# A decoder layer on one core: the order of the first loads, the place of attention's constants, and when the clearing of slots begins

## The chip, the cores and the metric

The kernel runs on one NeuronCore of a Trainium2 chip. A core has five engines with a queue each: PE (TensorE, matmuls; the load of its weights is shown as PEld), DVE (VectorE), ACT (ScalarE), POOL (GpSimd) and SP (SyncE, which here only hands out transfers). Sixteen DMA engines move the data. The metric is the time of one execution on the device in microseconds, lower is better. The span is the time from the first to the last instruction of the profiled execution.

## The reference

Input x has 8 sequences of 512 tokens with 512 numbers each, all in float32; a context of the same shape and a mask come with it. Three sublayers follow each other, and after each its output is added to its input and normalised without parameters:

```
x = norm(x + ssm(x))         # state space layer
x = norm(x + xattn(x, ctx))  # cross-attention, 16 heads of 32
x = norm(x + moe(x))         # 32 experts, 4 per token, plus a shared MLP
```

The state space layer is what matters for the beginning. It normalises x with ln_w and ln_b, multiplies by in_proj_w (512 x 2048) into a main half and a gate z, convolves each of the 1024 channels over four tokens (conv_w, conv_b) and applies SiLU. x_proj_w makes of that a step size dt and the vectors B and C of 16 states. Then, for each channel and state, `h = exp(A dt) h + dt B x`, with `A = -exp(A_log)`, runs over all tokens of the sequence, and `y = sum(h C) + D x` is gated with SiLU(z), multiplied by out_proj_w and by res_scale, and added to x.

Cross-attention projects with Wq, Wk, Wv, Wo and the biases bq, bk, bv, bo; masked positions get a score of -1e8. The experts each take at most 640 tokens (CAP): a token's rows go into slots, and rows beyond are dropped.

## The kernel before

The program has three parts after one another: `layers` (state space layer, attention and gate), `experts`, and `finish` (the last norm).

`layers` works in 16 chunks of T = 256 tokens, two for each sequence (`chunks`). Within a chunk there are 32 steps (`steps`, counted by k): four pairs of channel blocks q, four groups of states g, two blocks. A step makes decays on ACT (`decays`, L438), multiplies on DVE with a broadcast of B (`scan`, L450), scans on DVE (L454), multiplies with a broadcast of C (`collect`, L471) and sums over states on PE (L475). The broadcasts are the tiles `bc`, which SP fetches from a small scratch in DRAM (`bcast`, L379). Into these steps the code weaves other work by their number k: the output of the chunk before (`back`), the gate's projection (`gate_x`), the next chunk's input (`load_x` at k = 5, `norm_x` at 9, `flip_x`, `convolve`, `x_proj`), and a list `side` of attention's work for the sequence before, popped by weights.

Before the first chunk's steps there is a front with nothing to weave it into: load x, normalise it (`norm_x`), transpose (`flip_x`), four times project and convolve (`convolve`, with the matmuls in `project`, L303, the copy in L323 and the taps in L329 and L337), SiLU, the projection to dt, B and C (`x_proj`, L360, spilled to DRAM by L368), the preparation of dt (`prepare`), its spreading to both halves of the partitions (L419), the broadcasts, and the first decays.

The weights of the projections come in pieces of 512 KB through three buffers (`wm`, from the generator `pieces`). Its first `next` asks for two pieces and gives the first; every later one asks for one more and gives the one asked for before. In `before` the generator starts in the first `project`.

Constants are loaded by `const` (L128), one transfer on SP's queue each, and A_log by 16 small transfers (L149). `aneg` is made of it on ACT and DVE (L153, L154). Attention's constants follow: bq is scaled (L166), qa, ka and va get rows of ones and zeros (L206 to L213), the mask becomes a fill (L217 to L221), and bv goes through Wo into bo: a copy of bv's columns (L974), eight matmul instructions in the profile (L975), a sum (L978). `clear` (L235 to L240) writes one expert's 640 slots from a tile `zero` with one transfer of 1362.5 KB; it is called 32 times, at every odd k of the first two chunks (L1091). All transfers named here are on SP's queue.

The code's order is not the order on the engines. When the program is built, a planner runs it against assumed costs: each engine takes, whenever it is idle, the ready instruction that stands first in the program. An instruction is ready when its inputs are there and its buffer is free. The order that results is fixed for the chip, where each engine then keeps to it and waits where an input is late. `keep_in_program_order` holds the SiLUs and their table loads in the order written.

Of the kernel before, what the change touches and what calls it, by code (L numbers as in the profile page):

```python
# [1 line left out]

# [14 lines left out]
P = 128  # L17
# [9 lines left out]
T = 256  # L27
# [54 lines left out]
def layers(ctx, tc, a, x1d, filld, based, xbuf):  # L82
# [48 lines left out]
    def rows(w):  # L131
        return w.rearrange("(c p) f -> p c f", p=P)

    lnw = const("lnw", [P, DC], a["ln_w"])
    lnb = const("lnb", [P, DC], a["ln_b"])
    cw = const("cw", [P, CC, 4], rows(a["conv_w"]))
# [8 lines left out]
    for r in range(2):  # L145
        for j in range(2):
            for g in range(NST // NG):
# [17 lines left out]
    bq = const("bq", [P, DC], a["bq"])  # L165
    nc.vector.tensor_scalar(bq, bq, HD**-0.5, None, ALU.mult)  # L166
    bk = const("bk", [P, DC], a["bk"])
    bv = const("bv", [P, DC], a["bv"].rearrange("(c p) -> p c", p=P))
    bo = const("bo", [P, D], a["bo"].partition_broadcast(P))
    wg = const("wg", [P, DC, E], rows(a["wg"]))  # L170


    ones = cp.tile([P, P], F32, name="l_ones")
# [38 lines left out]
    va = cp.tile([P, SC, NH // 2, 3 * HD], F32, name="l_va")  # L212
    nc.gpsimd.memset(va[:, :, :, HD : 2 * HD], 1.0)  # L213


    mu8 = p3.tile([P, D], F32, tag="row", name="mu8").bitcast(U8)[0:B, 0:S]
    nc.sync.dma_start(mu8, a["mask"])  # L217
    fl = p3.tile([P, D], F32, tag="row", name="fl")
    nc.vector.tensor_copy(fl[0:B, :], mu8)
    nc.vector.tensor_scalar(fl[0:B, :], fl[0:B, :], -1.0, 1e8, ALU.add, ALU.mult)  # L220
    nc.sync.dma_start(filld, fl[0:B, :])  # L221

    def big(tag, name):
        return p1.tile([P, SC * (ROW if tag == "s1" else D)], F32, tag=tag, name=name)

# [14 lines left out]
        )  # L240

    def pieces():


        w_in, w_out = rows(a["in_proj_w"]), rows(a["out_proj_w"])
        xs = [w_in[:, :, 2 * q * P : 2 * (q + 1) * P] for q in range(CC // 2)]
        zs = [w_in[:, :, DI + 2 * q * P : DI + 2 * (q + 1) * P] for q in range(CC // 2)]
        outs = [w_out[:, 2 * q : 2 * q + 2, :] for q in range(CC // 2)]  # L250
        n = B * (S // T)
        order = list(xs)
        for i in range(n):
            order += (outs if i else []) + zs + (xs if i + 1 < n else [])
        order += outs
        got = None
        for src in order + [None]:
            nxt = None
            if src is not None:
                nxt = p2.tile([P, 4 * 2 * P], F32, tag="wm", name="wm", bufs=3).rearrange(  # L260
                    "p (c f) -> p c f", c=src.shape[1]
                )
                nc.sync.dma_start(nxt, src)
            if got is not None:
                yield got
            got = nxt
# [440 lines left out]
    def units(b):  # L707
# [258 lines left out]
                add(*sends[j])  # L966
        return todo


    load("Wo")  # L970
    rep = p3.tile([P, D], F32, tag="row", name="rep")
    psb = psm.tile([P, D], F32, tag="mm", name="ps_bo")
    for dc in range(DC):
        nc.vector.tensor_copy(rep[:, dc * P : (dc + 1) * P], bv[:, dc : dc + 1].to_broadcast([P, P]))  # L974
        nc.tensor.matmul(  # L975
            psb, rep[:, dc * P : (dc + 1) * P], loaded["Wo"][:, dc, :], start=(dc == 0), stop=(dc == DC - 1)
        )
# [40 lines left out]
    do(prepare, 0, f)  # L1018
    dry()
    bc, n = bcast(f, 0), 0  # L1020
    decays(0, 0, f["ready", 0][0], das[0])
    old, side = None, []

    for i, (b, t) in enumerate(chunks):
        nf = {}
        after = chunks[i + 1] if i + 1 < len(chunks) else None
        if t == 0:
            side, spent = units(b - 1) if b else sources(0), 0.0

            own = [work(k) for k in range(len(steps))] * 2  # L1030
            whole = sum(own) + sum(x[0] for x in side)
        py = None
        for k, (q, g, ci) in enumerate(steps):
            if ci == 0:
                if (q, g) != (CC // 2 - 1, NST // NG - 1):
                    bcn = bcast(f, (g + 1) % (NST // NG))
                else:
                    bcn = bcast(nf, 0) if after else None
            h = carry(t, 2 * q + ci, g)

            if k + 1 < len(steps) or after:
# [24 lines left out]
            if after:  # L1066
                if k == 5:
                    load_x(*after, nf)
                if k == 9:
                    norm_x(nf)  # L1070
                if k == 11:
                    for j in range(DC // 2):
                        do(flip_x, j, nf)
                if k in (12, 15, 18, 21):
                    do(convolve, after[1], (k - 12) // 3, nf, first=(k == 12))
                if k == 23:
                    dry()
                    silu(*nf["xs"].values())
                if k == 24:
                    do(x_proj, nf)  # L1080
            if side and (k >= 3 or t and k == 0):
                at = t * len(steps) + k + 1
                while side and spent + sum(own[:at]) <= whole * at / len(own):
                    w, fn, alone = side.pop(0)
                    spent += w
                    do(fn, first=alone)
            settle()
            collect(2 * q + ci, g, h, bc, py, f)
            if ci == 1:
# [330 lines left out]
```

## Time and profile before

| | |
|---|---|
| median of three runs | 5591.53 us (5585.55 to 5597.78) |
| profiled execution | 5587.21 us, span 5585.2 us |
| granted PE clock | 0.938 of full speed |
| PE busy | 4864.8 us (87% of the span) |
| DVE busy | 4348.3 us (78%) |
| ACT busy | 2589.2 us (46%) |
| moved by DMA | 769.83 MB, 138 GB/s on average |

The profile is one execution. Its slices cut the span into 40 equal stretches of 140 us; a digit is the busy share of an engine in tenths. In a timeline, a line gives start and duration in us, engine, line of the code, operation, what it writes and reads, and how many alike were merged; in brackets stands how long the engine was idle before, and what ended that. For a transfer ("SPq") the duration is that of handing it out on SP, not of the movement. In a view of waits, the numbers are us in total, times, and the longest.

### The profile page before, as it was taken

The numbers are of one execution on the slowest core, as the hardware profiler recorded it, in microseconds if no ns is written. First come the engines' busy times: TensorE is split into PE (matmuls) and PEld (weight loads), VectorE is DVE, ScalarE is ACT, GpSimd is POOL, SyncE is SP. The second block draws the span as 40 slices with busy tenths as digits, with TensorE's granted clock in tenths as the row PEclk, the third lists the DMA queues.
The fourth block names the chain that finished last, engine by engine and source line by source line (L and its number), as shares of the span: only waits on it lengthen the run. The fifth ranks groups of instructions, "written<-read, shape, count | busy, mean of one in ns | idle before, by whom it ended". The sixth has DMA issues, their size and how long they took to land. (4 is left out here: it accounts for less than half of the span.)

```text
span 5585.2 us, 60354 instructions
## 1 busy us (share of the span) xinstructions
PE 4864.8 (87%) x19752; PEld 2711.8 (49%) x19752; DVE 4348.3 (78%) x5738; ACT 2589.2 (46%) x5481; POOL 565.5 (10%) x424
## 2 busy tenths in 40 slices
PE   5667888888988988888888898889899999999994
PEld 3233344334433434443443343333577777777773
DVE  5998999999889999898989999853566565555554
ACT  4554655565566555565555656523222222222223
POOL 0000002001100200200010020010111111111111
PEclk8778999999999999999999999989999999999997
DMA  7787345444634634543463464431445545454444
GB/s 202 214 230 203 106 130 183 123 115 134 187 105 112 199 103 127 180 129 109 128 199 101 116 189 111 113 118 37 140 124 126 125 125 125 119 126 125 123 115 139
DMA packets 560426, 769.83 MB, mean 138 GB/s; under 512 B 135754, under 2 KB 268394, under 8 KB 560112
## 3 DMA queue, kind: packets, MB, share of 16 engines
q1 hardware_dynamic: 522608, 680.70, 41.6%
q0 software_dynamic: 33280, 76.90, 7.3%
q10 hardware_dynamic: 4224, 8.39, 0.4%
q8 instruction: 156, 2.56, 0.2%
q14 instruction: 158, 1.29, 0.1%
HBM read 508.68 MB, written 165.05 MB: 121 GB/s over the span
## 5 line engine op out<-in xcount | busy, mean ns | idle before, releaser
L438 ACT ACTIVATE l_da<-both,l_aneg 128x256 f32<-128x256 f32 x2048 | 889.1, 499 | 816.9 <-DVE h L454 775.4
L454 DVE TENSOR_TENSOR_SCAN h<-l_da,h 128x1028 f32<-128x1028 f32 x512 | 1169.8, 2292 | 51.6 <-ACT h L444 29.6
L475 PE MATMUL py<-h,l_twice 128*64 128x256 f32 x4096 | 625.4, 419 | 210.5 <-DVE h L471 210.3
L450 DVE TENSOR_TENSOR h<-both,bc 128x1024 f32<-128x1024 f32 x512 | 617.8, 1214 | 134.4 <-PE py L475 72.0
L471 DVE TENSOR_TENSOR h<-h,bc 128x1024 f32<-128x1024 f32 x512 | 622.4, 1218 | 8.2 <-DMA bc<-scr 2.1
L475 PEld LDWEIGHTS py<-h,l_twice 128*64 128x64 f32 x4096 | 292.5, 146 | 585.9 <-DVE h L471 251.0
L767 PE MATMUL ps_s<-l_ka,l_qa 64*128 64x512 f32 x1024 | 319.3, 703 | 141.7 <-DVE mx L769 141.3
L1200 PE MATMUL ps_h<-xT,w 128*128 128x320 f32 x1536 | 436.1, 434 | 0.0
L1280 POOL DMA_INDIRECT based<-y,xe x160 | 252.2, 1577 | 1314.3 <-ACT y L1303 573.8
L769 DVE TENSOR_REDUCE mx<-ps_s 128x2 f32<-128x1024 f32 x256 | 310.1, 1214 | 82.7 <-PE ps_s L767 81.8
L1221 DVE TENSOR_TENSOR hT<-ps_h,p 128x320 f32<-128x320 f32 x128 | 62.9, 491 | 374.9 <-PE ps_h L1200 374.7
L1200 PEld LDWEIGHTS ps_h<-xT,w 128*128 128x128 f32 x1536 | 292.5, 191 | 118.4 <-issue 0.8
L793 PE MATMUL ps_t<-l_qa,l_ka 64*128 64x512 f32 x1024 | 298.0, 646 | 15.8 <-ACT eT L797 12.1
L797 ACT ACTIVATE eT<-ps_t 128x1024 f32<-128x1024 f32 x256 | 258.7, 1012 | 109.5 <-PE ps_t L793 109.3
L809 PE MATMUL po<-eT,l_va 128*64 128x512 f32 x1024 | 279.2, 623 | 24.4 <-ACT raw L821 19.6
L1200 PE MATMUL ps_h<-t,s 128*128 128x320 f32 x1024 | 286.1, 432 | 0.0
L642 POOL DMA_INDIRECT xbuf<-x2t,dest x128 | 218.3, 1706 | 651.2 <-DVE dest L636 561.8
L704 PE MATMUL ps_p<-x2T,wa 128*128 128x512 f32 x512 | 245.5, 629 | 12.9 <-DVE hT L884 10.7
L303 PE MATMUL ps_z<-xnT,wm 128*128 128x256 f32 x1024 | 240.9, 388 | 15.4 <-DVE o L513 13.0
L303 PE MATMUL ps_x<-xnT,wm 128*128 128x256 f32 x1024 | 240.8, 389 | 3.2 <-ACT dt L401 1.9
L504 PE MATMUL po<-wm,zs 128*128 128x512 f32 x512 | 233.3, 605 | 3.3 <-DMA wm<-in_out_proj_w 1.8
L1200 PEld LDWEIGHTS ps_h<-t,s 128*128 128x128 f32 x1024 | 194.6, 190 | 81.1
(225 smaller groups left out, 7401.3 us busy)
## 6 DMA issues: line engine op xcount, KB each, us to landing
bc<-scr SPq DMA_DIRECT2D x1024, 128.0 KB
w<-in_w SPq DMA_DIRECT2D x96, 1024.0 KB
wm<-in_in_proj_w SPq DMA_DIRECT2D x128, 512.0 KB
xbuf<-zero SPq DMA_DIRECT2D x32, 1362.5 KB
xe<-xbuf SPq DMA_DIRECT2D x32, 1362.5 KB
both<-dt SPq DMA_DIRECT2D x256, 128.0 KB
both<-dtx SPq DMA_DIRECT2D x256, 128.0 KB
wm<-in_out_proj_w SPq DMA_DIRECT2D x64, 512.0 KB
```

The lines of the kernel that those rows point to most:

```text
L303: nc.tensor.matmul(ps[:, i, :], w[:, dc, i * P : (i + 1) * P], f["xnT"][:, dc, :], start=(dc == 0), stop=(dc == DC - 1),)
L438: nc.scalar.activation(da[:, n, 1:], dt[:, c % 2, j, :], AF.Exp, scale=aneg[:, c, j, g, m : m + 1])
L450: nc.vector.tensor_tensor(steps, dtx[:, c % 2].unsqueeze(2).to_broadcast([P, 2, NG // 2, T]), bc[0], ALU.mult)
L454: nc.vector.tensor_tensor_scan(flat, da.rearrange("p n t -> p (n t)"), flat, 0.0, ALU.mult, ALU.add)
L471: nc.vector.tensor_tensor(steps, steps, bc[1], ALU.mult)
L475: nc.tensor.matmul(py[j * HP : (j + 1) * HP, c % 2, :], twice, h[:, j * 2 + m, 1:], start=False, stop=(s == (NST // NG - 1, NG // 2 - 1, 1)),)
L767: nc.tensor.matmul(ps[:, j, :], qa[r, lt * P : (lt + 1) * P], ka[r, :], start=True, stop=True)
L769: return lambda: nc.vector.tensor_reduce(mx[:, lt, :].unsqueeze(2), ps, AX.X, ALU.max) and None
L793: nc.tensor.matmul(ps[:, j, :], ka[r, kc * P : (kc + 1) * P], qa[r, :], start=True, stop=True)
L797: nc.scalar.activation(eT, ps, AF.Exp)
L809: nc.tensor.matmul(po[j * 2 * HD : (j + 1) * 2 * HD, :], va[:, kc, i, j * HD : (j + 2) * HD], eT[:, j, :], start=(kc == 0), stop=(kc == SC ...
L1200: nc.tensor.matmul(ps, w[:, n, r * P : (r + 1) * P], x[:, n, :], start=not more and n == 0, stop=n == 1, skip_group_check=more,)
```

## The change

Four things move; no instruction's work changes.

1. x of the first chunk is the first transfer, and the generator of weight pieces is started right after it (`begun`), so that two pieces of in_proj_w come second and third. All constants follow, attention's five (bq to wg) directly behind A_log. The first chunk uses the tile loaded so.
2. `aneg` is made after the first broadcast, before the first decays.
3. The scaling of bq, the mask's fill and the product of bv and Wo go into a function `biases`, called in step 2 of the first chunk; Wo is loaded in step 0.
4. The clearings begin when seven steps of the first chunk are over, and are spread evenly over the rest of the first two chunks, up to its end.

```diff
+    def begun(it):
+        first = next(it)
+        return chain([first], it)
+
+    x0 = p1.tile([P, NT_, D], F32, tag="xt", name="xt")
+    nc.sync.dma_start(x0, a["x"][0, 0:T, :].rearrange("(j p) d -> p j d", p=P))
+    piece = begun(pieces())
     lnw = const("lnw", [P, DC], a["ln_w"])
...
-    nc.scalar.activation(aneg, aneg, AF.Exp)
-    nc.vector.tensor_scalar(aneg, aneg, -1.0, None, ALU.mult)
...
     bq = const("bq", [P, DC], a["bq"])
-    nc.vector.tensor_scalar(bq, bq, HD**-0.5, None, ALU.mult)
     bk = const("bk", [P, DC], a["bk"])
...
-    mu8 = p3.tile([P, D], F32, tag="row", name="mu8").bitcast(U8)[0:B, 0:S]
-    nc.sync.dma_start(mu8, a["mask"])
-    fl = p3.tile([P, D], F32, tag="row", name="fl")
-    nc.vector.tensor_copy(fl[0:B, :], mu8)
-    nc.vector.tensor_scalar(fl[0:B, :], fl[0:B, :], -1.0, 1e8, ALU.add, ALU.mult)
-    nc.sync.dma_start(filld, fl[0:B, :])
...
-    piece = pieces()
...
-    load("Wo")
-    rep = p3.tile([P, D], F32, tag="row", name="rep")
-    psb = psm.tile([P, D], F32, tag="mm", name="ps_bo")
-    for dc in range(DC):
-        nc.vector.tensor_copy(rep[:, dc * P : (dc + 1) * P], bv[:, dc : dc + 1].to_broadcast([P, P]))
-        nc.tensor.matmul(
-            psb, rep[:, dc * P : (dc + 1) * P], loaded["Wo"][:, dc, :], start=(dc == 0), stop=(dc == DC - 1)
-        )
-    nc.vector.tensor_tensor(bo, bo, psb, ALU.add)
+    def biases():
+
+        nc.vector.tensor_scalar(bq, bq, HD**-0.5, None, ALU.mult)
...
-    f = {}
-    load_x(0, 0, f)
+    f = {"xt": x0}
     norm_x(f)
...
     bc, n = bcast(f, 0), 0
+    nc.scalar.activation(aneg, aneg, AF.Exp)
+    nc.vector.tensor_scalar(aneg, aneg, -1.0, None, ALU.mult)
     decays(0, 0, f["ready", 0][0], das[0])
-    old, side = None, []
+    old, side, cleared = None, [], 0
...
+            if i == 0 and k == 0:
+                load("Wo")
+            if i == 0 and k == 2:
+                biases()
...
-            if i < 2 and k % 2:
-                clear(i * E // 2 + k // 2)
+            while i < 2 and cleared < E * (i * len(steps) + k - 6) // (2 * len(steps) - 7):
+                clear(cleared)
+                cleared += 1
```

In `biases`, the lines on the mask and on bv follow as they stood before.

More of the change, by code (lines that the diff above doesn't have):

```diff
@@ L1 @@
 from contextlib import ExitStack
+from itertools import chain
 import concourse.bass as bass
@@ L132, in rows, with pieces @@
         return w.rearrange("(c p) f -> p c f", p=P)
+    def pieces():
+        w_in, w_out = rows(a["in_proj_w"]), rows(a["out_proj_w"])
+        xs = [w_in[:, :, 2 * q * P : 2 * (q + 1) * P] for q in range(CC // 2)]
+        zs = [w_in[:, :, DI + 2 * q * P : DI + 2 * (q + 1) * P] for q in range(CC // 2)]
+        outs = [w_out[:, 2 * q : 2 * q + 2, :] for q in range(CC // 2)]
+        n = B * (S // T)
+        order = list(xs)
+        for i in range(n):
+            order += (outs if i else []) + zs + (xs if i + 1 < n else [])
+        order += outs
+        got = None
+        for src in order + [None]:
+            nxt = None
+            if src is not None:
+                nxt = p2.tile([P, 4 * 2 * P], F32, tag="wm", name="wm", bufs=3).rearrange(
+                    "p (c f) -> p c f", c=src.shape[1]
+                )
+                nc.sync.dma_start(nxt, src)
+            if got is not None:
+                yield got
+            got = nxt
+    def begun(it):
[4 more added lines that the diff above has]
+    piece = begun(pieces())
     lnw = const("lnw", [P, DC], a["ln_w"])
@@ L152, in layers @@
                 )
-    nc.scalar.activation(aneg, aneg, AF.Exp)
-    nc.vector.tensor_scalar(aneg, aneg, -1.0, None, ALU.mult)
+    bq = const("bq", [P, DC], a["bq"])
+    bk = const("bk", [P, DC], a["bk"])
+    bv = const("bv", [P, DC], a["bv"].rearrange("(c p) -> p c", p=P))
+    bo = const("bo", [P, D], a["bo"].partition_broadcast(P))
+    wg = const("wg", [P, DC, E], rows(a["wg"]))
     conv_tail = cp.tile([P, CC, 3], F32, name="l_conv_tail")
@@ L163, in layers @@
         nc.gpsimd.memset(da[:, :, 0:1], 0.0)
-    bq = const("bq", [P, DC], a["bq"])
-    nc.vector.tensor_scalar(bq, bq, HD**-0.5, None, ALU.mult)
[L167 to L170, printed above, removed]
     ones = cp.tile([P, P], F32, name="l_ones")
@@ L240, in clear @@
         )
[L244 to L261, printed above, removed]
-                )
[L263 to L266, printed above, removed]
-    piece = pieces()
     def load_x(b, t, f):
@@ L967, in units @@
         return todo
-    load("Wo")
-    rep = p3.tile([P, D], F32, tag="row", name="rep")
-    psb = psm.tile([P, D], F32, tag="mm", name="ps_bo")
-    for dc in range(DC):
-        nc.vector.tensor_copy(rep[:, dc * P : (dc + 1) * P], bv[:, dc : dc + 1].to_broadcast([P, P]))
-        nc.tensor.matmul(
-            psb, rep[:, dc * P : (dc + 1) * P], loaded["Wo"][:, dc, :], start=(dc == 0), stop=(dc == DC - 1)
-        )
-    nc.vector.tensor_tensor(bo, bo, psb, ALU.add)
+    def biases():
+        nc.vector.tensor_scalar(bq, bq, HD**-0.5, None, ALU.mult)
+        mu8 = p3.tile([P, D], F32, tag="row", name="mu8").bitcast(U8)[0:B, 0:S]
+        nc.sync.dma_start(mu8, a["mask"])
+        fl = p3.tile([P, D], F32, tag="row", name="fl")
+        nc.vector.tensor_copy(fl[0:B, :], mu8)
+        nc.vector.tensor_scalar(fl[0:B, :], fl[0:B, :], -1.0, 1e8, ALU.add, ALU.mult)
+        nc.sync.dma_start(filld, fl[0:B, :])
+        rep = p3.tile([P, D], F32, tag="row", name="rep")
+        psb = psm.tile([P, D], F32, tag="mm", name="ps_bo")
+        for dc in range(DC):
+            nc.vector.tensor_copy(rep[:, dc * P : (dc + 1) * P], bv[:, dc : dc + 1].to_broadcast([P, P]))
+            nc.tensor.matmul(
+                psb, rep[:, dc * P : (dc + 1) * P], loaded["Wo"][:, dc, :], start=(dc == 0), stop=(dc == DC - 1)
+            )
+        nc.vector.tensor_tensor(bo, bo, psb, ALU.add)
     chunks = [(b, t) for b in range(B) for t in range(S // T)]
```

## The prediction, made before the changed kernel was run

> **What bounds the kernel now.** I read the cores view first (one core, span 5585.2 us, granted clock 0.938), then the page's slices, then timelines of one engine at a time over the first 480 us, since every edit lies there. The slices (each digit a tenth of busy time in 140 us):
>
> ```profile
> PE   5667888888988988888888898889899999999994
> DVE  5998999999889999898989999853566565555554
> DMA  7787345444634634543463464431445545454444
> ```
>
> Slice 1 of DVE is half empty and the next ones are full. So the start is a front in which everything waits; then DVE carries chunk after chunk until about 3740 us, and PE the experts after that. The DMA share is highest in the first four slices, where the clearings of slots run. The front in SP's timeline (start, duration, line, transfer, count):
>
> ```profile
> 0.81 0.40 SPq L128 DMA_DIRECT2D l_lnw<-in_ln_w  x1
> 5.34 10.91 SPq L149 DMA_DIRECT2D l_aneg<-in_A_log  x16
> 19.01 4.13 SPq L208 DMA_DIRECT2D l_ka<-l_ones  x6
> 24.14 0.42 SPq L526 DMA_DIRECT2D wa<-in_Wo  x1
> 26.14 0.39 SPq L272 DMA_DIRECT2D xt<-in_x  x1
> 26.58 1.85 SPq L263 DMA_DIRECT2D wm<-in_in_proj_w  x3
> 28.52 3.66 SPq L237 DMA_DIRECT2D xbuf<-zero  x2
> ```
>
> SP hands out 0.4 to 0.7 us per transfer, one after another; x is handed out only at 26.14. DVE's and ACT's timelines show who waits for it:
>
> ```profile
> 31.79 1.29 DVE L73 BATCH_NORM_STATS2 st<-xt 128x6 f32<-128x512 f32 x2 [5.49 <-DMA xt<-in_x]
> 41.97 0.59 ACT L323 COPY xp<-ps_x 128x512 f32<-128x512 f32 x1 [2.90 <-PE ps_x L303]
> 50.25 0.59 ACT L323 COPY xp<-ps_x 128x512 f32<-128x512 f32 x1 [2.37 <-DVE xs L337]
> 55.49 0.59 ACT L323 COPY xp<-ps_x 128x512 f32<-128x512 f32 x1 [3.47 <-DVE xs L337]
> 81.87 2.36 DVE L450 TENSOR_TENSOR h<-both,bc 128x1024 f32<-128x1024 f32 x2 [8.16 <-DMA bc<-scr]
> ```
>
> So: x lands at 31.79; the four convolutions follow at 41.97, 46.11, 50.25 and 55.49; the first scan step begins at 81.87. From there DVE hardly stops. The waits view of DVE from 84 to 270 us, whole:
>
> ```profile
> DVE zs L487 <- PE py L475: 2.4, 2, 2.0
> DVE h L454 <- ACT l_da L438: 0.2, 1, 0.2
> ```
>
> From 270 to 460 it waits 15 us, of that 0.8 for a transfer (xt). So the clearings cost DVE nothing, and a start of the first scan that is so much earlier moves all that follows: nothing later is tied to a clock.
>
> **What the Trainium skill says.** "DMA: Bandwidth & Descriptors", the section on the anatomy of one DMA, gives about 2.0 us plus bytes at 436 GB/s, for GpSimd's transfers; 512 KB would take an estimated 3.2 us. This trace: the 256 KB of `based` and Wo's 1 MB behind it, handed out from 23.74, are used at 29.89 (6.15 us for 1.25 MB); x, 512 KB more, at 31.79. That is 1.9 us per 512 KB and 1.4 us besides, 3.3 us for one piece alone; it agrees. The same page, "Issuing engines are not separate DMA queues", says that all share 16 engines and interleave, so a big transfer ahead delays a small one. "PSUM — Partial Sum Buffer", "Engine vs sequencer instructions", says that ScalarE's, VectorE's and GpSimd's queues are strictly first in, first out, and that matmuls keep program order. That decides what a badly placed bias matmul holds up.
>
> **The change part by part.**
>
> *x and two weight pieces first.* x goes out at 0.81 and lands 3.3 us later, at 4.1, 27.7 us earlier. From x to the first convolution's copy are 41.97 − 31.79 = 10.18 us, so 14.3; the second follows 4.14 us later, at 18.4. The constants that norm and convolution need (lnw, lnb, cw, cb) are handed out by about 5 and land in time.
>
> *The third piece.* Only two pieces go first; the third is asked for in the second projection, behind all constants. SP's queue ahead of it: x 0.43 and two pieces 0.62 each (1.67 us), then what ran from 0.81 to 23.19 (the constants, 16 for A_log, attention's five, six rows of ones: 22.38 us), then `based` 0.40. Mask, fill and Wo no longer stand ahead. So it goes out at 0.81 + 1.67 + 22.38 + 0.40 = 25.3. In the waits view of SP over the first 900 us (total, times, longest), issues wait for older transfers:
>
> ```profile
> SPq L379 <- DMA xbuf<-zero: 22.4, 10, 4.1
> ```
>
> If the ninth to eleventh transfers wait likewise for x and the two pieces (landing at 4.1, 6.0 and 7.9), the queue slips by up to 1.85 us; I take half, so 26.2, landing at 29.5. The trace of before can't show this wait; both ends are 28.6 and 30.5. Its 16 matmuls take 3.72: copy at 33.2 instead of 50.25. The fourth piece is right behind. Before, the fourth copy was 5.24 us after the third, 1.1 of it behind the next chunk's statistics; now 4.14 to 5.24. It stands at 37.4 to 38.5 instead of 55.49: **17.0 to 18.1 us earlier, I take 17.5**. Some 10 of the 27.7 us stay behind the constants.
>
> *Wo and the bias product in chunk 0.* SP, PE, DVE and ACT are not in program order here: clearings that belong to step 1 and step 3 of chunk 0 went out at 28.52, before the first projection. A planner fills an idle engine with whatever is ready, first in the program first. So I expect the biases again in the front. DVE pays 0.16 + 0.41 + 0.41 + 0.61 + 0.69 = 2.28 us (L166, L219, L220, L974, L978). Their cover is DVE's idle time in the front, now above all from 18 to 30 us, and then between convolutions. Without cover all 2.28 fall on the full DVE; I take 0.5, as one instruction may get in the way. PE pays 8 matmuls, 5.48 us (L975). The gap between the fourth projection's end (55.45) and the x-projection (59.26) is 3.8 us; they overhang by 1.7, or by one matmul of 0.7 if the x-projection takes precedence. I take 0.5, between nothing (other gaps) and 1.7. What the matmul is queued ahead of is the x-projection, and everything waits for that.
>
> *aneg's exponential and negation* (0.31 + 0.23) move behind the broadcast; A_log lands at about 20, so idle ACT and DVE hide them, 0.54 if not. The memsets of GpSimd start within its first 11 us as before, needed later. Nothing.
>
> *Clearings.* The same 32 transfers of 1362.5 KB, from step 8 of chunk 0 on, in 57 steps instead of 64; the rates go from one in 2.0 steps to one in 1.8. They are first needed by the scatter of sequence 0's tokens, two chunks later. SP's slow hand-outs (3.66 us for two at 28.52) stood in front of pieces that weren't wanted until 41.97. Cover: the broadcasts are there before DVE wants them. Nothing, with a loss possible (fourth rival).
>
> Sum: 17.5 − 0.5 − 0.5 = **16.5 us**. The profiled execution took 5587.2 (its span and 2.0 us): 5570.7. The median of the runs shown is 4.3 us above it, so I forecast 5575.0.
>
> **Rivals.**
> *The whole shift.* The third piece isn't held up (the planner puts it ahead of constants). Then 27.7 − 1.0 = 26.7 us, 5565. Against: before, SP kept to program order in everything that was ready.
> *PE stands behind the bias matmuls.* Wo now follows three pieces of 512 KB: handed out at about 28, behind 1.5 MB from 26.2: 1.4 + 2.5 MB at 1.9 us per 512 KB = 10.9, landing at 37. If the planner puts the bias matmuls ahead of the fourth projection, that waits till 37 and 5.48 more, 42.6 instead of 33.2; its copy comes 8.9 us later than reckoned. If only ahead of the x-projection, 2 us. Gain about 8: 5583. For: PE can't overtake. Against: the planner knows sizes.
> *The new order gives it back.* Every instruction is planned anew. Against: the pairs of chunks repeat, by SP's hand-outs of x1d, within 2 us (467.5, 468.3, 466.7, 467.8, 468.7); for: the first pair takes 477.9. Gain near 0 to 5: 5589.
> *Slower: broadcasts late behind clearings.* In chunk 1 some 18 clearings instead of 16, at a DMA share of already 0.81 (280 to 460 us). SP waited up to 4.1 us for a clearing without DVE noticing; were DVE's lead used up, each such broadcast would cost 4.1 us. From 16.5 / 4.1, four of them, the gain is gone; from seven on it is slower by more than 0.2% (28.7 − 16.5 = 12.2 us). At ten, 5616. Against: in chunks 0 and 1 no step after the first waited for a broadcast.
>
> **How the numbers follow.** Forecast 0.60 (gains of 12 to 21), whole shift 0.10, PE behind the biases 0.14, given back 0.10, slower 0.06. A measurement of this kernel can tell about 0.2%, 11.2 us, from no change. Faster by more: 0.60 + 0.10 = 0.70; within: 0.14 + 0.10 = 0.24; slower: 0.06. The range of 5564 to 5586 takes in the first three cases, 0.84, with their unknown costs (the slip of 1.85, the overhang, the DVE work); the part outside is the last two.
>
> **What would show it.** x's statistics at about 4 us on DVE; the third piece on SP at 25 to 27 and PE's third projection waiting for it; the fourth copy at about 38; the first multiplication of a step at about 65 instead of 81.87; from there DVE without waits for broadcasts, x1d going out some 16 us earlier in every chunk. Wrong if PE waits for Wo ahead of a projection, if the third piece goes out before the constants, if DVE waits for bc among clearings, or if pairs of chunks change their length.

## The result, and the profile after

The changed kernel takes 5574.55 us, the median of 8 runs (5557.79 to 5579.9), beside 5591.13 us (5585.55 to 5597.78) for the kernel before: a ratio of 0.9965 (of the means), 95% interval 0.9956 to 0.9975; the medians lie 16.6 us apart. It is faster by more than the 0.2% that can be told from no change. Run again beside other kernels (the last experiment) it gave 0.9955 (0.9938 to 0.9971). Its profiled execution took 5579.9 us (span 5578.2), the longest of its runs. The forecast was 5575.0 us. The time was met; the way to it was not, as will be seen: the front gave less than the sum said, and, by the profiles, a part that was priced at nothing made up for it.

The page's slices of the changed kernel (columns as before):

```profile
PE   6768889889888988888888898889899999999994
DVE  6988899999889999898989999854565556555554
DMA  6787455445534634543463464431444444454544
```

DVE's first slice rose from 5 to 6. The shape is otherwise the same, so the change has to be read in the timelines. SP's, of the changed kernel (start, duration of the hand-out, line, transfer, count):

```profile
0.81 0.44 SPq L166 DMA_DIRECT2D xt<-in_x  x1
1.31 1.00 SPq L154 DMA_DIRECT2D wm<-in_in_proj_w  x2
...
3.91 1.68 SPq L129 DMA_DIRECT2D l_cb<-in_conv_b  x1
...
6.11 1.31 SPq L129 DMA_DIRECT2D l_w_dt<-in_dt_proj_w  x1
...
8.89 10.91 SPq L183 DMA_DIRECT2D l_aneg<-in_A_log  x16
...
22.56 4.13 SPq L239 DMA_DIRECT2D l_ka<-l_ones  x6
...
27.24 1.58 SPq L154 DMA_DIRECT2D wm<-in_in_proj_w  x3
28.86 0.50 SPq L523 DMA_DIRECT2D wa<-in_Wo  x1
...
38.04 0.46 SPq L260 DMA_DIRECT2D xbuf<-zero  x1
```

x goes first, and the third piece of weights (first of the three at 27.24) stands behind every constant. SP was held up on the way there: two constants took 1.68 and 1.31 us to hand out instead of 0.58 each, while x and the pieces were still moving. Wo was pulled into the front. So was a clearing, at 38.04: the seven steps in the code did not keep four of the 32 clearings out of the time ahead of the first step. DVE's and ACT's timelines:

```profile
4.76 1.29 DVE L74 BATCH_NORM_STATS2 st<-xt 128x6 f32<-128x512 f32 x2 [4.76 <-DMA xt<-in_x]
17.48 0.59 ACT L320 COPY xp<-ps_x 128x512 f32<-128x512 f32 x1 [5.03 <-PE ps_x L300]
37.72 0.59 ACT L320 COPY xp<-ps_x 128x512 f32<-128x512 f32 x1 [14.14 <-PE ps_x L300]
41.70 0.59 ACT L320 COPY xp<-ps_x 128x512 f32<-128x512 f32 x1 [2.21 <-DVE xs L334]
68.96 2.36 DVE L447 TENSOR_TENSOR h<-both,bc 128x1024 f32<-128x1024 f32 x2 [8.86 <-DMA bc<-scr]
```

x lands 27 us earlier than before, the first convolution's copy is 24.5 us earlier, the third and fourth only 12.5 and 13.8, and the first step 12.9. The hole of 14.14 us ahead of the third copy is the third piece. PE's timeline shows that hole too, and one thing more:

```profile
11.59 9.31 PE L300 MATMUL ps_x<-xnT,wm 128*128 128x256 f32 x32 [0.26 <-ACT xnT L289]
31.36 9.64 PE L300 MATMUL ps_x<-xnT,wm 128*128 128x256 f32 x32 [10.47 <-DMA wm<-in_in_proj_w]
...
52.98 3.70 PE L981 MATMUL ps_bo<-wa,rep 128*128 128x512 f32 x8
```

Two projections at two times 3.72 us would be 7.4; they took 9.3 and 9.6. The view of the tile ps_x in stretches of the changed kernel gives the time of one matmul (ns: least, median, longest; then when they started):

```profile
L300 PE MATMUL ps_x<-xnT,wm x4: 634/634/765, 31.4 to 32.8; 128*128 128x256 f32 x4
...
L300 PE MATMUL ps_x<-xnT,wm x21: 379/379/497, 36.2 to 40.6; 128*128 128x256 f32 x21
```

In the kernel before the same view at 38.2 us, where the projections started, reads:

```profile
L303 PE MATMUL ps_x<-xnT,wm x8: 379/379/483, 38.2 to 39.8; 128*128 128x256 f32 x8
```

After its pause of 10.5 us PE ran each matmul in 634 ns until 36.2, some 5 us, and only then in 379. The trace also records the clock granted to PE. A view of stretches of the changed kernel shows it (from and to; then length, busy time and count for these matmuls; granted clock; DMA share and GB/s):

```profile
31.00:36.40 5.40, 5.04 (x12) 0.50 1.04 359
36.40:41.00 4.60, 4.60 (x21) 1.00 0.73 223
```

So the slow matmuls are those at half the clock. In the kernel before, the clock stands at 1.00 over the projections from 38 to 53 us: the bias product (29.89 to 35.37) had run right ahead of them. The change took that away. The first projection of the changed kernel, where PE has just begun, is slow in the same way: its matmuls take 634 ns up to 15.6 us.

From the first step on, DVE's waits from 84 to 270 us, whole, for the changed kernel:

```profile
DVE h L447 <- DMA bc<-scr: 1.6, 1, 1.6
DVE zs L484 <- PE py L472: 1.4, 2, 0.9
DVE h L451 <- ACT l_da L435: 0.2, 1, 0.2
```

No wait here is large. The one of 1.6 us, at 257.85, is for a broadcast: the last four before it went out at 244.73 to 247.6, right behind a clearing (244.31). The two other profiles of this kernel, below, have 1.5 and 0.4 us there; the kernel before has no such wait. The end of chunk 0 comes 12.6 us earlier, much like the first step; it is read from the hand-out of x1d, the layer's output of a chunk, which SP writes to DRAM.

### The profile page after: what moved, and what is told of

Its sections match the earlier page's. It is cut to its first block, busy times and chain, and to the rows that moved or that the text cites. A ratio compares the mean times of both kernels' runs of the same rounds, so it can differ in the third digit from the quotient of the medians.

```text
span 5578.2 us, 60367 instructions
## 1 busy us (share of the span) xinstructions
PE 4883.5 (88%) x19752; PEld 2719.7 (49%) x19752; DVE 4347.7 (78%) x5738; ACT 2591.4 (46%) x5481; POOL 562.9 (10%) x424
## 5 line engine op out<-in xcount | busy, mean ns | idle before, releaser
L300 PE MATMUL ps_x<-xnT,wm 128*128 128x256 f32 x1024 | 245.8, 394 | 11.5 <-DMA wm<-in_in_proj_w 10.5
L701 PE MATMUL ps_p<-x2T,wa 128*128 128x512 f32 x512 | 243.8, 625 | 12.8 <-DVE hT L881 10.7
L1212 PEld LDWEIGHTS ps_h<-t,s 128*128 128x128 f32 x1024 | 194.6, 190 | 81.1
```

Of the source, the lines that this page charges most:

```text
L300: nc.tensor.matmul(ps[:, i, :], w[:, dc, i * P : (i + 1) * P], f["xnT"][:, dc, :], start=(dc == 0), stop=(dc == DC - 1),)
L1212: nc.tensor.matmul(ps, w[:, n, r * P : (r + 1) * P], x[:, n, :], start=not more and n == 0, stop=n == 1, skip_group_check=more,)
```

## The experiments

The table holds all profiles, in us: DVE's first step, SP's hand-out of x1d of chunks 0, 1 and 2, and the time between the last two, which is the stretch of chunk 2. The clearing rule is the one in the code, old (odd steps) or new.

| kernel | clearing | first step | x1d 0 | x1d 1 | x1d 2 | chunk 2 |
|---|---|---|---|---|---|---|
| before | old | 81.87 | 285.38 | 474.91 | 722.90 | 248.0 |
| before, again | old | 80.97 | 284.9 | 475.66 | 726.92 | 251.3 |
| x first alone | old | 88.72 | 290.7 | 479.79 | 729.84 | 250.1 |
| biases late alone | old | 77.27 | 283.7 | 474.77 | 723.34 | 248.6 |
| after, old clearing | old | 69.36 | 276.7 | 468.30 | 719.24 | 250.9 |
| after | new | 68.96 | 272.83 | 464.91 | 711.11 | 246.2 |
| after, again | new | 69.45 | 272.70 | 462.20 | 704.51 | 242.3 |
| after, third time | new | 68.25 | 271.68 | 463.26 | 706.74 | 243.5 |
| three pieces first | new | 67.73 | 274.6 | 466.18 | 709.52 | 243.3 |
| 60 warming matmuls | new | 68.25 | 275.0 | 466.76 | 707.60 | 240.8 |
| 38 warming matmuls | new | 68.92 | 272.47 | 463.11 | 707.08 | 244.0 |
| late constants | new | 53.78 | 263.6 | 455.17 | 699.64 | 244.5 |
| late constants, warm | new | 58.02 | 264.03 | 453.87 | 697.67 | 243.8 |
| clearings in chunk 1 | new place | 68.54 | 270.61 | 465.16 | 707.24 | 242.1 |

### x first alone

The kernel before, with x and two pieces first; the constants behind them in their old order, biases, aneg and clearings as they were.

```diff
+    x0 = p1.tile([P, NT_, D], F32, tag="xt", name="xt")
+    nc.sync.dma_start(x0, a["x"][0, 0:T, :].rearrange("(j p) d -> p j d", p=P))
+    piece = begun(pieces())
     (all constants, the mask's fill, Wo and the bias product as before)
-    piece = pieces()
-    load_x(0, 0, f)
```

> The kernel before with part 1 alone: x and two weight pieces first, everything else where it was, biases in the front included. My theory (the third piece behind the constants sets the front): mask, Wo and fill stand again ahead of the third piece, it goes out at about 28.5 us and lands behind Wo at 34 to 35; the bias matmuls run at about 33 and PE's third projection starts at about 39. First multiplication of a step (DVE, h<-both,bc) at 73 to 75 us, 5 later than in the changed kernel, 8 earlier than before; time 8 us under the kernel before. Rival (x first is the whole gain, the biases' place does nothing): first step at 69, 13 to 17 us under before.

Measured: 5595.25 us (12 runs) beside 5593.64, ratio 1.0007 (0.9998 to 1.0016). The first step came at 88.72, later than before, and neither expectation held. PE's timeline of this kernel:

```profile
34.35 5.72 PE L981 MATMUL ps_bo<-wa,rep 128*128 128x512 f32 x8 [34.35 <-DMA wa<-in_Wo]
39.91 0.60 PE L293 MATMUL ps_t<-l_ident,xt 128*128 128x128 f32 x4
```

The bias product is first in PE's fixed order, and it waits for Wo until 34.35; x had been there since about 4. x's transposes stand behind it, and the projections behind them. So the second rival of the prediction, PE behind the bias matmuls, is real, in the harshest form, when x alone is moved. Moving x first is worth nothing without moving the biases.

### The biases late alone

The kernel before, with part 3 alone.

```diff
-    (scaling of bq, mask's fill, load of Wo, bias product ahead of the first chunk)
+            if i == 0 and k == 0:
+                load("Wo")
+            if i == 0 and k == 2:
+                biases()
```

> The kernel before with part 3 alone: bq's scaling, mask, fill, Wo and the bias product in chunk 0. My theory: x goes out 2 us earlier and without Wo's 1 MB ahead, so it lands at about 28, 3.8 earlier; but the bias matmuls no longer run ahead of the first projection, so its first matmuls take 0.63 us instead of 0.38 for about 4 us, and 2.2 of it are lost. First step at 79 to 81 us instead of 81.87, time within 0.1% of before. Rival (the biases in the front were what held up the front): first step at 76 or earlier.

Measured: 5589.78 us (12 runs), ratio 1.0000 (0.9991 to 1.0009). PE's and DVE's timelines of this kernel:

```profile
34.51 15.40 PE L295 MATMUL ps_x<-xnT,wm 128*128 128x256 f32 x64 [0.47 <-ACT xnT L284]
...
77.27 2.36 DVE L442 TENSOR_TENSOR h<-both,bc 128x1024 f32<-128x1024 f32 x2 [6.88 <-DMA both<-dtx]
```

The first step is 4.6 us earlier, somewhat more than expected, and most of it is gone by the end of chunk 0 (1.7 us earlier). Here too the projections took 15.40 us for 64 matmuls where the kernel before took 14.08. With both parts, and the move of `aneg`, the first step comes about 12 us earlier (the next experiment), though neither alone gives a time that can be told from no change: each is held back by what the other removes. The move of `aneg` was not run alone; in the changed kernel ACT and DVE did that work at 23.28 and 25.55, in the hole ahead of the third copy.

### After, with the old clearing

```diff
-            while i < 2 and cleared < E * (i * len(steps) + k - 6) // (2 * len(steps) - 7):
-                clear(cleared)
-                cleared += 1
+            if i < 2 and k % 2:
+                clear(i * E // 2 + k // 2)
```

> The changed kernel with the clearings as before, one at each odd step from step 1 on. My theory (clearings cost nothing either way): first step at 68 to 70 us, DVE waits less than 3 us for broadcasts in chunks 0 and 1, ratio to before 0.9965 within 0.001, as the changed kernel. Rival (the later clearings bring part of the gain): first step at 71 or later, or a ratio of 0.998 or more.

Measured: 5576.71 us (7 runs), ratio 0.9974 (0.9962 to 0.9985), which overlaps with the changed kernel's 0.9965 and 0.9955. By times alone the clearing rule can't be told from nothing (by the medians 16.9 us under the kernel before, where the changed kernel has 16.6 and 22.6). The profile tells more. The first step is where it was (69.36), but the stretch of chunk 2, where no clearing is left to do, takes 250.9 us, as in all five profiles with the old rule (248.0 to 251.3, mean 249.8). The nine others, under the new rule or with the clearings in chunk 1, took 240.8 to 246.2, mean 243.4. DVE's timeline of this kernel in chunk 2:

```profile
483.57 2.36 DVE L468 TENSOR_TENSOR h<-h,bc 128x1024 f32<-128x1024 f32 x2 [1.89 <-DMA bc<-scr]
...
505.41 2.30 DVE L451 TENSOR_TENSOR_SCAN h<-l_da,h 128x1028 f32<-128x1028 f32 x1 [2.46 <-ACT h L441]
```

and of the kernel before:

```profile
490.40 2.36 DVE L471 TENSOR_TENSOR h<-h,bc 128x1024 f32<-128x1024 f32 x2 [2.11 <-DMA bc<-scr]
...
511.83 2.30 DVE L454 TENSOR_TENSOR_SCAN h<-l_da,h 128x1028 f32<-128x1028 f32 x1 [2.46 <-ACT h L444]
```

The same two waits are in the two other profiles with the old rule that stand alone (x first: 1.67 and 2.46; biases late: 2.82 and 2.47) and in before's second (1.86 and 2.46), and at these places in none with the new rule. SP's order at the start of chunk 2 shows the first of them. Before:

```profile
475.37 1.28 SPq L379 DMA_DIRECT2D bc<-scr  x2
...
488.12 0.94 SPq L263 DMA_DIRECT2D wm<-in_in_proj_w  x2
489.11 0.50 SPq L272 DMA_DIRECT2D xt<-in_x  x1
489.65 2.34 SPq L379 DMA_DIRECT2D bc<-scr  x3
```

and after:

```profile
465.38 2.57 SPq L376 DMA_DIRECT2D bc<-scr  x4
```

Before, two broadcasts went out ahead of dt's spreading and the rest came later, some behind weights and x; after, four went out at once. The second wait is ACT's reset of a column of h, which with the old rule stood behind a table load and two normalisations (1.28 and 1.52 us). So the clearing rule does change chunk 2, not through DMA traffic, as no clearing goes out there, but through the order: the planner, handed a program with the clearings at other places, settled on another one two chunks later. Why it chose that order was not traced. The two waits are most of the 5.6 us between the two kernels in chunk 2; DVE's busy time differs by about 1.

### Three pieces first

The changed kernel, with the third piece ahead of the constants as well.

```diff
-        first = next(it)
-        return chain([first], it)
+        first = [next(it), next(it)]
+        return chain(first, it)
```

> The changed kernel with three weight pieces ahead of the constants instead of two. My theory: PE's third projection follows the second without a pause (copy at about 25.7 us instead of 37.72), and now the fourth piece is the one behind the constants: out at about 28, landing at 31.5, after a pause of PE with slow matmuls again; fourth copy at 37 to 38 instead of 41.70. First step at 64 to 66 us, 4 us earlier than the changed kernel; ratio to before 0.9955 to 0.9965. Rival (another constant or A_log sets the front by now): first step stays at 68 to 69.

Measured: 5579.09 us (6 runs), ratio 0.9970 (0.9958 to 0.9983), and the first step at 67.73. Copies stood at 18.77, 22.90, 27.04 and 39.54. PE's timeline of this kernel:

```profile
33.50 5.87 PE L300 MATMUL ps_x<-xnT,wm 128*128 128x256 f32 x16 [7.86 <-DMA wm<-in_in_proj_w]
```

The hole has only moved from the third projection to the fourth. The generator asks for a piece when the one before is taken, so the last piece waits behind the constants whichever it is; and its matmuls are slow ones after the pause. The gain of 10.7 us at the third copy is 2.2 us at the fourth and 1.2 at the first step, less than the 64 to 66 us expected. The piece went out at 29.34, later than the 28 expected, since SP took longer over the constants.

### Late constants

The three pieces first, and A_log's 16 transfers, res_scale, attention's five, the rows of ones and the zeros of `based` moved behind the four convolutions in the program.

```diff
     (x, three pieces, lnw to dpar)
-    rs, aneg's 16 transfers, bq, bk, bv, bo, wg, ones, qa, ka, va, based
     ... four convolutions of chunk 0
+    rs, aneg's 16 transfers, bq, bk, bv, bo, wg, ones, qa, ka, va, based
```

> The changed kernel with three weight pieces first and with res_scale, A_log, attention's five constants, the rows of ones and based's zeros moved in the code behind the first chunk's convolutions; only the eight constants that the front needs stay ahead of them. My theory (constants on SP's queue hold the third and fourth piece): the convolutions run at their own pace of 4.1 us, copies at about 18, 22, 26 and 30 us; first step at 54 to 58 us, 11 to 15 earlier than in the changed kernel. If what the front gains is gained in full, the time is 24 to 28 us under the kernel before (ratio 0.995 to 0.9957). Rival (later chunks give gains back, since work like the next chunk's statistics loses its idle place in the front): first step at 54 to 58 but a ratio of 0.9965 or more.

Measured: 5571.58 us (4 runs) beside 5593.01, ratio 0.9958 (0.9941 to 0.9975). Copies at 16.38, 20.51, 24.65 and 28.79, and DVE's timeline of this kernel has its first step 28.1 us earlier than the kernel before:

```profile
53.78 2.36 DVE L385 TENSOR_TENSOR h<-both,bc 128x1024 f32<-128x1024 f32 x2 [3.50 <-DMA both<-dtx]
```

So the constants ahead of the last pieces were what held the front of the changed kernel. But x1d of chunk 0 comes only 21.8 us earlier: 6.3 are lost in chunk 0 itself. DVE now has the next chunk's statistics to do there (202.0 us busy in its stretch instead of some 200), which the waiting front had covered; the larger part, 4.3 us, is more waiting, 3.8 of it for two broadcasts (at 187.80 and 248.61). Its time can't be told from the changed kernel's, and the ratio lies just above the range expected.

### Warming matmuls

The changed kernel with 60 extra matmuls of the identity between the second and third projection, to keep PE running until the third piece lands (each is two matmul instructions in the profile), and later with 38.

```diff
+        if q == 1:
+            pw = psy.tile([P, 2, T], F32, tag="py", name="pw")
+            for _ in range(60):
+                nc.tensor.matmul(pw[:, 0, 0:P], ident, ident, start=True, stop=True)
```

> The changed kernel with 60 extra matmuls of the identity (128x128, their result not used) on PE between the second and the third projection, where PE waits 10 us for the third piece. My theory (PE's matmuls take 0.63 instead of 0.38 us for about 4 us after a pause): the third projection's 16 matmuls take 3.7 us instead of 6.4, third copy at about 35 instead of 37.72 and first step at 66 to 67 instead of 68.96. Rival (the slow matmuls have to do with late weights, not with the pause): 6.4 us again, first step at 69.

> The changed kernel with 38 extra matmuls of the identity between the second and the third projection instead of 60, which ran 2.3 us over the arrival of the third piece. My theory: they end at about 29.5, the third projection starts when its weights land at 31.4 and takes 3.7 us; third copy at 35 to 35.5 instead of 37.7 to 38.0, fourth at 39 to 40, first step at 66 to 67.5 instead of 69 to 69.5. Rival (something else sets the first step): the third copy moves and the first step stays at 69.

One run each: 5571.65 and 5572.2 us, first steps at 68.25 and 68.92. PE's timeline with 60:

```profile
20.49 13.34 PE L1022 MATMUL pw<-l_ident 128*128 128x128 f32 x118
33.66 7.07 PE L300 MATMUL ps_x<-xnT,wm 128*128 128x256 f32 x32
```

and with 38:

```profile
19.97 8.42 PE L1022 MATMUL pw<-l_ident 128*128 128x128 f32 x74
31.32 8.83 PE L300 MATMUL ps_x<-xnT,wm 128*128 128x256 f32 x32 [2.92 <-DMA wm<-in_in_proj_w]
```

Without a pause, the two projections take 7.07 us instead of 9.64, nearly all matmuls at 379 ns and none slower than 382, and the granted clock stays at 1.00 (20 to 41 us). That shows that the slowness comes from the idle time and not from the data or the transfers beside it. But 60 ran 2.3 us past the landing (31.36 in the changed kernel), so what they saved was spent. With 38 they ended 2.92 us too soon, and that pause was enough: the matmuls took 634 ns again until about 34.7 (granted clock 0.50 from 31.5 to 34.8), and the third copy came at 36.86 rather than the expected 35.0 to 35.5. The fourth copy was 0.85 us earlier than in the changed kernel, yet the first step was not: one of the hand-outs of dtx took 1.42 us instead of 0.6, so the broadcasts behind it went out at 65.06, as against 65.27. A gain of 1 us in the front can vanish in SP's queue.

### Late constants, and PE warmed

The late constants with 22 identity matmuls while x is on its way.

```diff
+    pw = psy.tile([P, 2, T], F32, tag="py", name="pw")
+    for _ in range(22):
+        nc.tensor.matmul(pw[:, 0, 0:P], ident, ident, start=True, stop=True)
```

> The kernel with late constants (three pieces first, constants behind the convolutions) and 22 extra matmuls of the identity on PE while x is on its way, result not used. My theory (the first 4 us of matmuls after a pause are slow, wherever they are): the first projection's 16 matmuls take 3.7 us instead of about 5, first copy at 15.3 instead of 16.38, fourth at about 27.8 instead of 28.79; first step at 52 to 54, since a new order of broadcasts and spreads can cost or bring 1 to 3 us; ratio to before 0.9945 to 0.9965. Rival (slow at the start whatever ran before): first copy at 16.4.

Measured: 5565.5 us (4 runs) beside 5591.23, ratio 0.9957 (0.9940 to 0.9974). The expectation failed: copies at 16.89, 21.02, 28.70 and 32.84, first step at 58.02. The first projection was no faster; between the end of the warming at 8.5 us and the first projection at 11.44, PE was busy for only 1.3 us, with transposes, and its matmuls took 634 ns again (granted clock 0.50 from 11.7 to 15.0). The later copies were late for another reason, in DVE's timeline:

```profile
26.32 0.17 DVE L910 TENSOR_SCALAR l_bq<-l_bq 128x4 f32<-128x4 f32 x1 [3.50 <-DMA l_bq<-in_bq]
26.39 1.67 DVE L276 SCALAR_TENSOR_TENSOR xs<-xp,l_cw,xs 128x256 f32<-128x256 f32 x4
```

The scaling of bq (0.17 us) now stood in the middle of the second convolution, and DVE waited 3.50 us for bq to land with the convolution's taps behind it. This is the prediction's "one instruction may get in the way" at seven times the 0.5 us set down for it. x1d of chunk 0 came 21.4 us earlier nonetheless, as with the late constants, and the time is the same. Neither of the two is shown to beat the changed kernel.

### Both kernels once more

The two kernels unaltered, to see how far one execution's profile can be trusted.

> The changed kernel once more, to see how two executions of the same program differ. My theory: the front is the same to 0.5 us (first step at 69), and what differs from the first profile arises in chunks 3 to 15 and in the experts, by several us either way, with the granted clock. Rival (the order planned anew loses the gain in these chunks): the hand-outs of x1d lose their lead over before from 11 to 4 us again, in the same chunks.

> The kernel before once more, for the same purpose: first step at 81.9 to 0.5 us, x1d of chunk 5 within 3 us of 1420, of chunk 15 within 8 us of 3741. Rival: chunk by chunk the same to 1 us.

Measured: 5567.75 us (span 5566.0) for the changed kernel, 12.2 less than its first profile's span, with the first step at 69.45 instead of 68.96; 5592.68 for the kernel before (span 5589.9), 4.7 more, with its first step at 80.97. So the front repeats within 1 us in these pairs, though before's first step and its x1d of chunk 5 (1423.7) fell outside the ranges set down, and the rest varies by nearly as much as the whole change. By the sixteenth x1d, the first profile of the changed kernel is 3.9 us ahead of the first of before, the second 17.2 ahead. A reading of one pair of profiles past the front can be wrong by 10 us.

### Clearings in chunk 1, and the changed kernel a third time

```diff
-            while i < 2 and cleared < E * (i * len(steps) + k - 6) // (2 * len(steps) - 7):
-                clear(cleared)
-                cleared += 1
+            if i == 1:
+                clear(k)
```

> The changed kernel with all 32 clearings of slots in chunk 1, one per step, none in chunk 0; everything is computed. Theory (clearings are hidden wherever they stand): DVE's first step stays within 1 us of 68.96, DVE's waits for broadcasts in chunks 0 and 1 stay below 3 us in all, and the ratio to the kernel before stays at 0.9965 within 0.0015. Rival A (the four clearings that still went out ahead of the first step delay it): without them the first step begins 2 us or more earlier, at 67 or less. Rival B (the fourth rival of the prediction, broadcasts behind clearings): chunk 1 now moves 32 clearings instead of some 19, at a DMA share that was 0.85 there already; DVE waits 10 us or more for broadcasts in chunk 1, and the ratio is 0.9985 or more.

> The changed kernel unaltered, beside the run with the clearings in chunk 1 on the same chip. Expected: ratio to the kernel before 0.9965 within 0.001, DVE's first step at 69 within 0.5, as in the two profiles of it so far. The rival that the gain beyond the front's 12.9 us was chance puts the ratio at 0.9977 (12.9 us of 5591).

Measured: 5572.76 us (7 runs) with all clearings in chunk 1, ratio 0.9971 (0.9960 to 0.9983), and 5568.22 (4 runs) for the changed kernel, 0.9955 (0.9938 to 0.9971). The intervals overlap. The first step with two clearings in the front instead of four is at 68.54, within the spread of the changed kernel's three (68.25 to 69.45), so the clearings in the front cost less than can be seen. In chunk 1 the DMA share rose to 0.91 (270 to 460 us), as against 0.82 to 0.85. SP's waits from 250 to 500 us with all clearings in chunk 1 (total, times, longest):

```profile
SPq L376 <- DMA xbuf<-zero: 13.3, 6, 5.6
```

and DVE's from 270 to 500 us, its whole answer:

```profile
DVE k L686 <- PE ps_p L701: 7.0, 1, 7.0
DVE xs L334 <- ACT xs L326: 5.7, 1, 5.7
DVE zs L484 <- PE py L472: 5.7, 3, 2.6
DVE dtx L407 <- ACT dtx L403: 5.5, 1, 5.5
DVE st L74 <- DMA xt<-in_x: 2.5, 1, 2.5
DVE m L60 <- ACT r L58: 0.5, 1, 0.5
```

Six broadcasts were held up by clearings, one by 5.6 us, and DVE never waited for a broadcast. The fourth rival's mechanism was driven further than the change drives it in chunk 1 and did not bite. Chunk 1 did take 194.6 us in this profile, the longest of the fourteen (189.1 to 192.1 in the others). DVE's waits there are for PE and ACT; whether the clearings cost these 2.5 us or more in another way is not shown.

## Why the prediction was right, and where it was wrong

**The order on SP, right in kind, short in size.** x at once, the third piece behind all constants, Wo in the front: as forecast. The piece went out at 27.24, where 26.2 was forecast with ends at 25.3 and 27.2; the slip was 1.9 us rather than half of that. It took 4.1 us to be used, not 3.3. x took 3.95, a piece of the kernel with three first 4.2 and one of the late constants, warm, 4.1. So "lands 3.3 us later" was low by 0.7 to 0.9. The estimate from the Trainium skill, "DMA: Bandwidth & Descriptors", the section on one DMA's anatomy, of 3.2 us was low with it; the measurement decides. Together 1.9 us.

**The failed step: "Its 16 matmuls take 3.72".** They took 6.4, since PE had been idle for 10.5 us and its clock was at half. This alone is 2.6 of the miss. The Trainium skill had it: "TensorE: Matmul & The Clock Gate", Part 1 on the HAM clock gate, says that PE runs at half its clock until it has been busy for about 3.4 us, and falls back after about as long a window without work. The granted clock of this trace agrees: 0.50 up to 36.4 us, 1.00 from there. The matmuls last 634 ns and then 379; their starts are 427 and then 216 ns apart, a factor of two. On the length of the pause the runs differ: 2.92 us were enough after the 38 warming matmuls. The prediction read a duration from a place in the kernel before where PE was warm, and put it where PE would be cold. The bias product in the front of before was counted as a cost, 5.48 us of PE, and had also been the warm-up of the projections behind it. The first copy, forecast for 14.3, came at 17.48 for the same reason, 0.7 of it being x's later landing; the wait for the third piece hid that.

**From the fourth copy to the first step, right in size by chance.** Fourth after third: 3.98 us (4.14 to 5.24 forecast). Then 27.26 us to the first step instead of 26.38, 0.9 more, where 1.0 was reckoned for the biases on PE and DVE. But the biases cost hardly anything: the last product before the spreading starts 17.70 us after the fourth copy instead of 17.53, although the bias matmuls (3.70 us on PE between dt's matmuls and the gate's) and the addition on DVE stand in between. The larger part, 0.7, is one hand-out. A broadcast of B consists of two transfers. Before, the first of them went out ahead of dt's spreading:

```profile
68.29 0.52 SPq L379 DMA_DIRECT2D bc<-scr  x1
...
78.89 8.27 SPq L379 DMA_DIRECT2D bc<-scr  x13
```

and in the changed kernel both behind it:

```profile
65.27 8.89 SPq L376 DMA_DIRECT2D bc<-scr  x14
```

The step starts 3.0 us after the hand-out of the second one, before (78.89) and after (65.91). In the kernel with 60 warming matmuls, which has the biases at the same place, one transfer again goes out early (56.17), and the stretch from the fourth copy to the first step is 26.47 us. The prediction had also misread the gap ahead of the x-projection: the fourth projection ends at 52.30 and not at 55.45, so PE is idle there for 6.96 us and not for 3.8, and nothing overhangs. So the first step stands at 68.96 instead of about 65.4: 1.9 + 2.6, less 0.8 for the closer fourth copy and 0.1.

**The sum for the front: 16.5 forecast, 12.5 measured** (means of two profiles before, 81.42, and three after, 68.89).

**"Clearings: nothing" failed too, in the other direction.** The stretch of chunk 2 took 249.6 us before (mean of two) and 244.0 after (mean of three): 5.6 us. The old rule put back into the changed kernel brings the long stretch back, with its two waits of together 4.1 to 5.3 us. After chunk 2 the changed kernel leads by 17.5 us, at the sixteenth x1d by 14.4 (means of the same profiles); the medians of the times show 16.6 and 22.6. That only the front's 12.9 us were gained, a ratio of 0.9977, lies outside both intervals of the changed kernel (up to 0.9975 and 0.9971). Still, the 5.6 us are shown in the profiles of chunk 2 alone: the times of the kernel with the old rule do not show that they are missing. How the gain is spread beyond chunk 2 is not settled either, since executions of one kernel differ there by 10 us and more. So, as far as the profiles show, the forecast time was met by luck: the front gave 4 us less than forecast, and chunk 2 some 5 that the forecast did not have.

**The rivals.** The whole shift did not occur; it is near to what the late constants did at the first step, of which a quarter was given back in chunk 0. PE behind the bias matmuls did not occur in the change but did as soon as x alone was moved. "The new order gives it back" named the right mechanism, a planner that arranges everything anew, with the wrong sign: in chunk 2 the new order gave 5.6 us more. Broadcasts late behind clearings cost little: 0.4 to 1.6 us once in chunk 0 in the three profiles of the changed kernel, and nothing in chunk 1, even with all clearings there.

## What to carry to other kernels

Take a matmul's duration from a place where PE has been as busy, or as idle, as it will be in the new place; after a pause of 3 us or more allow for 3.4 to 5 us at the slow rate, and look at the granted clock of the stretch. Where a queue's order is fixed ahead, a move pays only if everything that stood ahead of it on every engine moves too: look for the first instruction of each queue and what that waits for. And where a planner orders the whole program, an edit's side effect can appear chunks away, so compare the waits of the whole stretch in more than one profile of each kernel before crediting the edit's own place.

## What was not expected of the hardware

- After a pause of 10.5 us, a matmul of 128x256 in float32 took 634 ns for some 5 us and 379 from then on. After a pause of 2.92 us it was slow for 3.4 us; without a pause it was never slow.
- It is not the length of the pause that decides. The skill's same part says that a window of about 3.4 us decides, which runs freely, so that its phase varies. The clock records of these traces fit that: the half clock lasts 10.24 us in the changed kernel (26.17 to 36.41), 3.41 with 38 warming matmuls (31.46 to 34.87) and 3.42 in the late constants, warm (11.66 to 15.08), all close to multiples of 3.41. In the 3.41 us ahead of the last two PE was busy for 0.49 and 1.78 us. In the kernel before, the two stretches of 3.41 us from 33.53 to 40.35, which take in the bias product's end and 1.3 us of transposes, have 2.52 and 2.74 us of busy time, and the clock stayed at 1.00. How much busy time is enough is not settled.
- A transfer of 512 KB took 3.95 to 4.65 us from the start of its hand-out to its use, the longest with three pieces handed out right behind it.
- Handing out a small constant took 0.43 us, but for two of them 1.3 to 3.0, depending on the kernel, while x and the pieces were under way.
